# A graph layer with bucketed edges: the first and the last level of ranks as two levels of 64 ranks each

## The chip, the cores and the metric

One core of one Trainium2 chip runs the kernel. The metric is the device time of one execution in microseconds (us), the median of several runs. Engines are named as the profile names them: PE (TensorE matmul) and PEld (its weight loads), DVE (VectorE), ACT (ScalarE), POOL (GpSimd), SP (SyncE, which issues most DMAs).

## The reference

12,500 nodes with 64 features; 212,500 edges (100,000 random pairs in both directions and a loop at each node), sorted by `dst`. `h` is the layer norm of `x` with a relu. For every edge

```
e = silu(silu([h[src], h[dst], dist] @ eW1 + eb1) @ eW2 + eb2)      # 129 -> 128 -> 128
```

The sums of `e` over the edges of one source node form `agg`, and the output is

```
x + silu([h, agg] @ nW1 + nb1) @ nW2 + nb2
```

All of it is float32.

## The kernel before

The edges come sorted by `dst`, but the sums go by `src`. So the kernel sorts them into buckets through DRAM. Node `l * 100 + b` belongs to bucket `b` of 100, and a bucket has 125 nodes. Four buckets are a quad (`G = 4`); there are 25 quads.

**Sending.** The edges are taken in 208 blocks of 1024. For each block, `count` finds on DVE and PE which rank each edge has within its bucket (running totals stand in the PSUM tile `full`), and `send` makes the part of the first layer that belongs to `dst` and the distance (matmul `qp`, L427; copies to `qs` on ACT, L437 and L443). Eight indirect DMAs a block, issued by POOL (L450), then scatter the rows to the DRAM array `q`: a row of 144 floats for each edge (128 values, then the place of its source node within the bucket), at quad, rank, bucket. A block goes out in three pieces (`PIECES`). `qs` has eight buffers, two a block.

**Levels.** Each bucket has room for 2304 ranks. `LEVELS` cuts them into levels: an entry `(n, end, spare)` is a level of n x 128 ranks for every bucket, which is full when block `end` has been sent. `spare` slots of it may be left empty and are zeroed (`fill`); later rows of a bucket that is behind are then moved past the level's end. There are 12 levels: the first is `(1, 18, 0)`, the last `(1, 208, 128)`.

**Steps.** When a level is full, its rows are read back quad by quad (`fetch`: one DMA for `qt`, one for `a`, the table rows of the quad's nodes; four buffers each, `NQ = 4`). A level with n = 2 takes two steps for a quad, one with n = 1 takes one. A step handles four tiles of 128 rows; where n = 1, tile t is bucket t of the quad. It consists of:

- `s_lr` (L526): the rows' node places, spread over partitions (PE, four bf16 matmuls); `s_one_t` (L531): the one-hot matrix `oneT` from them (DVE);
- `s_pt` (L540, L546): the rows turned by four transposes, and the source part `a` added through `oneT` by matmuls; then silu (ACT, L550). Each float32 matmul is two instructions on PE;
- `s_bias` and `s_p2` (L572, L578): the bias copied to PSUM (ACT), the second layer (PE), silu (ACT, L582);
- `s_one` (L559): the one-hot matrix `one` the other way round (DVE); at its end the next `fetch` is issued;
- `s_seg` (L592): the sums of the bucket by a matmul with `one`, into the PSUM tile `seg`, of which there is one buffer;
- `s_add` (L601, L603): `seg` copied or added to `aggT` (DVE).

There are 450 steps. After a quad's last step, `nodes` computes its output rows (`z`, L246 and L249; `o`, L255; `os`, L258) and SP stores them.

**Order.** PE, DVE, ACT and SP execute in the order in which the program is written; no scheduler moves anything. First come preparation and the first blocks. When all pieces of `goal_of(0)` are written, the loop over steps begins. One turn of it follows this list; the number is how many steps ahead (or back) each part works:

```
turn = [
    (s_pt, 1), (s_add, -2), (s_one_t, 2), None, (s_bias, 1), (s_p2, 0), (s_one, 0), None, (s_seg, -1), None, (s_lr, 3), None,
]
```

At each `None` (a hook) pieces of the sending, of the node tables still to be made (`feed`) and of finished quads are written. How many pieces of the sending are due is a straight line between marks; there is a mark at the first fetch of each level, by which the blocks of that level and three more must have been written:

```
LEAD = 3 * PIECES
total = PIECES * (nblocks - 2 * FIRST)
goal_of = lambda w: min(PIECES * (LEVELS[w][1] - 2 * FIRST) + LEAD, total)
```

With `FIRST = 4`, `goal_of(0)` is 39 pieces, which ends block 21; the total is 600. The first fetch of a level also waits on the chip for the landing of the level's last rows (`last_rows`).

Of the kernel before, what the change touches and what calls it, by code (L numbers as in the profile page):

```python
# [28 lines left out]
F32 = mybir.dt.float32  # L29
# [3 lines left out]
AF = mybir.ActivationFunctionType  # L33
OP = mybir.AluOpType
# [4 lines left out]
P = 128  # L39
L = 125  # L40
# [11 lines left out]
G = 4  # L52
W = 144
EPS = 1e-5

LEVELS = [(1, 18, 0), (1, 32, 0), (2, 58, 32), (2, 79, 96), (2, 101, 96), (2, 123, 96), (2, 145, 96), (2, 165, 128)]
LEVELS += [(1, 184, 0), (1, 194, 32), (1, 202, 96), (1, 208, 128)]
ENDS = [P * sum(n for n, _, _ in LEVELS[: w + 1]) for w in range(len(LEVELS))]
SURE = [end - spare for end, (_, _, spare) in zip(ENDS, LEVELS)]
ROWS = ENDS[-1]  # L60
CAP = ROWS // P
# [12 lines left out]
def tile_gnn(ctx: ExitStack, tc: tile.TileContext, x, src, dst, ew, eW1, eb1, eW2, eb2, nW1, nb1, nW2, nb2, out):  # L74
    nc = tc.nc
    N, D = x.shape
    H = eW2.shape[0]
# [97 lines left out]
    nc.vector.scalar_tensor_tensor(same, plus, -32.0, part, op0=OP.mult, op1=OP.add)  # L175
    nc.vector.tensor_scalar(plus, same, float(WL + 1), None, op0=OP.is_equal)
    nc.vector.scalar_tensor_tensor(same, plus, -1e6, same, op0=OP.mult, op1=OP.add)
    ones = const.tile([1, P], F32, name="ones")
    nc.vector.memset(ones, 1.0)
    before = const.tile([P, P], BF16, name="before")  # L180
# [88 lines left out]
    with ExitStack() as work:  # L269
# [199 lines left out]
        last_rows = {}  # L469
# [12 lines left out]


        batches = [(w, B, n) for w, (n, _, _) in enumerate(LEVELS) for B in range(NB // G)]
        steps = [(w, B, n, g) for w, B, n in batches for g in range(n)]
        PIECES = 1 + TB // G
        pending = [needed.count(w) for w in range(len(LEVELS))]
        batch, st = {}, {}

        most = max(n for _, _, n in batches)  # L490

        def fetch(i):
            if i >= len(batches):
                return
            c, B, n = batches[i]
            assert not any(pending[: c + 1])
            while B not in done_a:
                next(feed)
            at = B * G * ROWS + G * (ENDS[c] - n * P)
            qt = ld2.tile([P, G * most, W], F32, name="qt")  # L500
            ins = nc.sync.dma_start(
                qt[:, : G * n, :].rearrange("p j w -> p (j w)"),
                q[at : at + G * n * P, :].rearrange("(p j) w -> p (j w)", p=P),
            ).ins
            for later in range(c + 1, len(LEVELS)):
                tc.declare_no_dep(ins, group=f"rows{later}", reason="these ranks were full before")
            tc.add_manual_dep(ins, last_rows[LEVELS[c][1] - 1].name, AFTER)
            tc.add_to_no_dep_group("loads", ins)
# [19 lines left out]

        def s_one_t(k):
            oneT = wk.tile([L, G, P], F32, name="oneT")  # L530
            nc.vector.tensor_scalar(oneT, st[k].pop("lr")[:L], part1[:L, :], None, op0=OP.is_equal)  # L531
            st[k]["oneT"] = oneT

        def s_pt(k):

            (qt, a, _), tiles = of(k)
            oneT = st[k].pop("oneT")
            pt = mm.tile([P, G, P], F32, name="pt", tag="mm")
            for t, (j, _) in enumerate(tiles):
                nc.tensor.matmul(  # L540
                    pt[:, t, :], qt[:, j, :H], ident, is_transpose=True, start=t == 0, stop=False, skip_group_check=True
                )
            for b, same in itertools.groupby(range(G), lambda t: tiles[t][1]):
                same = list(same)
                cols = slice(same[0], same[-1] + 1)
                nc.tensor.matmul(  # L546
                    pt[:, cols, :], a[:L, b, :], oneT[:, cols, :], start=False, stop=True, skip_group_check=True
                )
            e1 = wk.tile([P, G, P], F32, name="e1")
            nc.scalar.activation(e1, pt, AF.Silu)  # L550
            st[k]["e1"] = e1

        def s_one(k):
            (qt, _, _), tiles = of(k)
            c, B, n, g = steps[k]
            wide = [P, G // n, n, L]
            loc = qt[:, : G * n, H : H + 1].rearrange("p (j b) w -> p b j w", b=G)
            one = wk.tile([P, G, L], F32, name="one")
            nc.vector.tensor_tensor(  # L559
                one.rearrange("p (b j) l -> p b j l", j=n),  # L560
                nodes1[:, None, None, :].to_broadcast(wide),
                loc[:, tiles[0][1] : tiles[0][1] + G // n].to_broadcast(wide),
                op=OP.is_equal,
            )
            st[k]["one"] = one
            if g == n - 1:
                fetch(c * (NB // G) + B + NQ)

        def s_bias(k):

            p2 = p2p.tile([P, G, H], F32, name="p2")
            nc.scalar.copy(p2, b2f)  # L572
            st[k]["p2"] = p2

        def s_p2(k):
            e1, p2 = st[k].pop("e1"), st[k].pop("p2")
            for t in range(G):
                nc.tensor.matmul(  # L578
                    p2[:, t, :], e1[:, t, :], w2, start=False, stop=t == G - 1, skip_group_check=True
                )  # L580
            e2 = wk.tile([P, G, H], F32, name="e2")
            nc.scalar.activation(e2, p2, AF.Silu)  # L582
            st[k]["e2"] = e2

        def s_seg(k):
            c, B, n, g = steps[k]
            item, tiles = of(k)
            if g == 0:
                item[2] = sgp.tile([P, G, L], F32, name="seg")
            e2, one = st[k].pop("e2"), st[k].pop("one")  # L590
            for t, (j, b) in enumerate(tiles):
                nc.tensor.matmul(item[2][:, b, :], e2[:, t, :], one[:, t, :], start=j < G, stop=j >= G * (n - 1))  # L592

        def s_add(k):
            c, B, n, g = steps[k]
            if g < n - 1:
                return
            v = aggT[:, B * G : B * G + G, :]
            seg = batch.pop((c, B))[2]
            if c == 0:  # L600
                nc.vector.tensor_copy(v, seg)  # L601
            else:
                nc.vector.tensor_tensor(v, v, seg, op=OP.add)  # L603
            if c == len(LEVELS) - 1:
                tails.append(nodes(B, *node_in.pop(B), mm, ndp[1], "mm"))
# [465 lines left out]
```

## Time and profile before

| | |
|---|---|
| median of 9 runs | 3059.62 us (3042.93 to 3077.78) |
| profiled execution | 3050.87 us, of which its span is 3049.0 us |
| granted TensorE clock, mean | 0.859 of full speed |
| busy share of the span | PE 76%, PEld 65%, DVE 64%, POOL 56%, ACT 36% |
| float32 matmul instructions of the steps | L546 2400, L578 3600, L592 3600 |
| indirect DMAs of the sending (L450) | 1661, on POOL 1691.9 us in all |
| reads of `qt` (L501) | 150 of 576 KB, 150 of 288 KB |

The profile gives, for each line and engine, the number of instructions, their busy time and what ended the idle time before them. A window view gives the same for a stretch of the span, with the granted clock and the DMA share. The span was seen to fall into these stages: preparation and the first blocks (0 to 281 us), steps with a dense stream of blocks (281 to about 773), the long middle, and the end, in which no block is sent any more (from about 2873).

### The profile page before, as it was taken

What the parts mean: (1) busy time and instruction counts of PE and PEld (TensorE: products, weight loads), DVE (VectorE), ACT (ScalarE), POOL (GpSimd) and SP (SyncE); (2) the same over time, 40 slices, a digit from 0 to 9 for tenths busy, and PEclk for the clock granted to TensorE, in tenths of its full rate; (3) what the DMA queues carried; (4) which work ended last, traced back from release to release, by engine and by line L of the source; (5) the groups of instructions that cost most, each with busy time, mean ns of one, the idle gap of its engine ahead of it and who ended that gap; (6) DMA issues with size and microseconds to landing.
All of it is one profiled execution on the core that took longest, in us unless ns stands there. A gap on an engine that the chain in (4) does not pass through costs nothing.

```text
span 3049.0 us, 46228 instructions
## 1 busy us (share of the span) xinstructions
PE 2305.2 (76%) x16191; PEld 1978.1 (65%) x16191; DVE 1955.4 (64%) x3005; ACT 1085.5 (36%) x2403; POOL 1721.0 (56%) x1712
## 2 busy tenths in 40 slices
PE   3754666555687777877777878887888888888997
PEld 2542565444576666666666766776776777778986
DVE  7654566555666666666667756666776677666643
ACT  2432222222233333333333333343444444334443
POOL 5666566666666566566566656655565665543210
PEclk9655787776799888898899888898999999989999
DMA  4543345444555544455443334333344444445652
GB/s 107 182 145 121 121 147 161 145 139 146 174 178 179 183 145 145 163 182 178 138 135 124 134 119 135 123 130 132 130 141 136 132 136 148 143 150 158 191 159 86
DMA packets 237005, 443.83 MB, mean 146 GB/s; under 512 B 49804, under 2 KB 108735, under 8 KB 236561
## 3 DMA queue, kind: packets, MB, share of 16 engines
q1 hardware_dynamic: 158629, 269.79, 28.0%
q0 software_dynamic: 53536, 123.03, 11.7%
q10 hardware_dynamic: 24602, 47.98, 5.3%
q8 instruction: 131, 2.15, 0.3%
q14 instruction: 107, 0.88, 0.1%
HBM read 251.07 MB, written 189.55 MB: 145 GB/s over the span
## 4 chain that ended last, share of the span: by engine, by line
PE 39%; issue 14%; DVE 13%; POOL 12%; another core or an unknown queue 9%; DMA 3%; ACT 2%; SPq 0%; POOLq 0%; DVEq 0%; ACTq 0%
POOL q L450 12%; PE seg L592 8%; PE p L578 8%; PE pt L546 8%; PE qp L427 5%; PE pt L540 4%; DVE each L362 2%; PE lr L526 2%; DVE oneT L531 2%; DVE oh L354 2%; DVE mine L402 2%; DVE one L559 1%; DVE aggT L603 1%; DVE rank L404 1%
## 5 line engine op out<-in xcount | busy, mean ns | idle before, releaser
L450 POOL DMA_INDIRECT q<-qs,to x1661 | 1691.9, 1019 | 1161.1 <-ACT qs L443 636.5
L592 PE MATMUL seg<-one,e 128*128 128x125 f32 x3600 | 550.3, 297 | 186.8 <-issue 77.2
L550 ACT ACTIVATE e<-pt 128x512 f32<-128x512 f32 x450 | 270.3, 601 | 1077.8 <-PE pt L546 310.2
L592 PEld LDWEIGHTS seg<-one,e 128*128 128x128 f32 x3600 | 487.0, 208 | 238.9 <-issue 190.5
L578 PE MATMUL p<-w,e 128*128 128x128 f32 x3600 | 546.1, 293 | 94.8 <-issue 53.4
L578 PEld LDWEIGHTS p<-w,e 128*128 128x128 f32 x3600 | 495.2, 204 | 165.6 <-issue 90.9
L531 DVE TENSOR_SCALAR oneT<-lr,part 125x512 f32<-125x512 f32 x450 | 336.0, 747 | 411.2 <-remote 160.9
L546 PE MATMUL pt<-oneT,a 125*128 125x128 f32 (+1 forms) x2400 | 526.4, 353 | 37.7 <-issue 34.7
L546 PEld LDWEIGHTS pt<-oneT,a 125*128 125x128 f32 x2400 | 392.6, 211 | 66.4 <-issue 44.7
L603 DVE TENSOR_TENSOR aggT<-aggT,seg 128x500 f32<-128x500 f32 x275 | 184.6, 671 | 342.8 <-remote 157.5
L437 ACT COPY qs<-qp 128x512 f32<-128x512 f32 x416 | 225.8, 589 | 482.0 <-PE qp L427 150.5
L582 ACT ACTIVATE e<-p 128x512 f32<-128x512 f32 x450 | 270.9, 602 | 239.6 <-remote 114.7
L427 PEld LDWEIGHTS qp<-win,pick 64*128 64x128 f32 x1662 | 186.6, 222 | 254.5 <-issue 200.6
L427 PE MATMUL qp<-win,pick 64*128 64x256 f32 x1662 | 310.5, 474 | 40.7 <-issue 27.4
L540 PE MATMUL pt<-ident,qt 128*128 128x128 f32 x1800 | 312.6, 300 | 29.8 <-issue 19.5
L362 DVE TENSOR_REDUCE each<-oh 128x100 bf16<-128x800 bf16 x208 | 315.4, 1516 | 7.2
L559 DVE TENSOR_TENSOR one<-nodes,qt 128x500 f32<-128x500 f32 x450 | 301.9, 671 | 0.0
L402 DVE TENSOR_TENSOR mine<-oh,full 128x800 f32<-128x800 bf16 x208 | 204.0, 981 | 112.0 <-remote 46.0
L572 ACT COPY p<-b2f 128x512 f32<-128x512 f32 x450 | 269.3, 599 | 0.0
L540 PEld LDWEIGHTS pt<-ident,qt 128*128 128x128 f32 x1800 | 213.6, 155 | 69.2 <-issue 46.9
L526 PE MATMUL lr<-identb,qt 128*125 128x128 bf16 x1800 | 199.1, 235 | 61.9 <-issue 42.7
L526 PEld LDWEIGHTS <-qt 128*125 128x125 bf16 x1800 | 173.3, 148 | 102.4 <-issue 89.6
(144 smaller groups left out, 1378.7 us busy)
## 6 DMA issues: line engine op xcount, KB each, us to landing
qt<-q SPq DMA_DIRECT2D x150, 576.0 KB
a<-ta SPq DMA_DIRECT2D x300, 256.0 KB
qt<-q SPq DMA_DIRECT2D x150, 288.0 KB
q<-zeros ACTq DMA_DIRECT2D x25, 1080.0 KB
q<-qs,to POOLq DMA_INDIRECT x1661
q<-zeros ACTq DMA_DIRECT2D x10, 1440.0 KB
bc<-dests SPq DMA_DIRECT2D x103, 128.0 KB
win<-tb SPq DMA_DIRECT2D x416, 30.0 KB
```

The costliest lines, as they stand in the source:

```text
L362: nc.vector.tensor_reduce(each, oh.rearrange("p t b -> p b t"), AX.X, OP.add)
L427: nc.tensor.matmul(qps[i][:, t, : n_of[t]], pick[at, t * P : (t + 1) * P], win[at, : n_of[t]], start=True, stop=True)
L450: ins = nc.gpsimd.indirect_dma_start(out=q[:], out_offset=bass.IndirectOffsetOnAxis(ap=to[:k, j : j + 1], axis=0), in_=qs[:k, t, a, :], in ...
L526: nc.tensor.matmul(lr[:L, t, :], loc[:, at : at + 1].to_broadcast([P, L]), identb, start=True, stop=True)
L531: nc.vector.tensor_scalar(oneT, st[k].pop("lr")[:L], part1[:L, :], None, op0=OP.is_equal)
L540: nc.tensor.matmul(pt[:, t, :], qt[:, j, :H], ident, is_transpose=True, start=t == 0, stop=False, skip_group_check=True)
L546: nc.tensor.matmul(pt[:, cols, :], a[:L, b, :], oneT[:, cols, :], start=False, stop=True, skip_group_check=True)
L550: nc.scalar.activation(e1, pt, AF.Silu)
L559: nc.vector.tensor_tensor(one.rearrange("p (b j) l -> p b j l", j=n), nodes1[:, None, None, :].to_broadcast(wide), loc[:, tiles[0][1] : ti ...
L578: nc.tensor.matmul(p2[:, t, :], e1[:, t, :], w2, start=False, stop=t == G - 1, skip_group_check=True)
L582: nc.scalar.activation(e2, p2, AF.Silu)
L592: nc.tensor.matmul(item[2][:, b, :], e2[:, t, :], one[:, t, :], start=j < G, stop=j >= G * (n - 1))
```

## The change

The first level becomes `(0.5, 11, 0), (0.5, 18, 0)`, the last `(0.5, 205, 64), (0.5, 208, 64)`: there are 14 levels. A level with n = 0.5 has 64 ranks of every bucket. A step of it takes one whole quad, 256 rows, in two tiles. Tile j holds bucket j on partitions 0 to 63 and bucket 2 + j on partitions 64 to 127. So `fetch` reads `qt` in two DMAs, one for each half of the partitions; `a` is read as before. `s_lr`, `oneT`, the transposes, the silus, the bias copy and the second layer work on two tiles instead of four. In `s_pt` the source part is added by four matmuls of 64 columns. For the sums, the new constant `nodes2` holds the node numbers on one half of the partitions and -1 on the other; so `one` has four blocks as before, each with zeros for the half of the partitions that belongs to another bucket, and `s_seg` keeps its four matmuls (two tiles, each used with two blocks of `one`). `s_add` and the fetch of `a` happen once for each level and quad, so for 50 quads more than before. `goal_of` is unchanged.

```diff
-LEVELS = [(1, 18, 0), (1, 32, 0), (2, 58, 32), (2, 79, 96), (2, 101, 96), (2, 123, 96), (2, 145, 96), (2, 165, 128)]
-LEVELS += [(1, 184, 0), (1, 194, 32), (1, 202, 96), (1, 208, 128)]
-ENDS = [P * sum(n for n, _, _ in LEVELS[: w + 1]) for w in range(len(LEVELS))]
+LEVELS = [(0.5, 11, 0), (0.5, 18, 0), (1, 32, 0), (2, 58, 32), (2, 79, 96), (2, 101, 96), (2, 123, 96), (2, 145, 96), (2, 165, 128)]
+LEVELS += [(1, 184, 0), (1, 194, 32), (1, 202, 96), (0.5, 205, 64), (0.5, 208, 64)]
+ENDS = [int(P * sum(n for n, _, _ in LEVELS[: w + 1])) for w in range(len(LEVELS))]
...
+    mid = const.tile([P, 2], F32, name="mid")
+    nc.vector.tensor_scalar(mid[:, 0:1], part, P / 2 - 0.5, None, op0=OP.is_lt)
+    nc.vector.tensor_scalar(mid[:, 1:2], part, P / 2 - 0.5, None, op0=OP.is_gt)
+    nodes2 = const.tile([P, 2, L], F32, name="nodes2")
+    for h in range(2):
+        nc.vector.tensor_scalar(nodes2[:, h, :], nodes1, 1.0, mid[:, h : h + 1], op0=OP.add, op1=OP.mult)
+    nc.vector.tensor_scalar(nodes2, nodes2, -1.0, None, op0=OP.add)
...
-        steps = [(w, B, n, g) for w, B, n in batches for g in range(n)]
+        steps = [(w, B, n, g) for w, B, n in batches for g in range(max(1, n))]
...
+            rows = G * int(n * P)
+            at = B * G * ROWS + G * ENDS[c] - rows
             qt = ld2.tile([P, G * most, W], F32, name="qt")
...
+            if n < 1:
+                parts = q[at : at + rows, :].rearrange("(r h j) w -> h r (j w)", h=2, j=2)
+                loads = [(qt[h * 64 : h * 64 + 64, :2, :], parts[h]) for h in range(2)]
+            else:
+                loads = [(qt[:, : G * n, :], q[at : at + rows, :].rearrange("(p j) w -> p (j w)", p=P))]
+            for to, part_ in loads:
+                ins = nc.sync.dma_start(to.rearrange("p j w -> p (j w)"), part_).ins
...
             c, B, n, g = steps[k]
+            if n < 1:
+                return batch[c, B], [(0, None), (1, None)]
...
-            nc.vector.tensor_scalar(oneT, st[k].pop("lr")[:L], part1[:L, :], None, op0=OP.is_equal)
+            nt = len(of(k)[1])
+            nc.vector.tensor_scalar(oneT[:, :nt], st[k].pop("lr")[:L, :nt], part1[:L, :], None, op0=OP.is_equal)
...
+            for j, h in itertools.product(range(nt), range(2)) if n < 1 else ():
+                cols = slice(h * 64, h * 64 + 64)
+                nc.tensor.matmul(
+                    pt[:, j, cols], a[:L, 2 * h + j, :], oneT[:, j, cols], start=False, stop=True, skip_group_check=True
+                )
...
+            if n < 1:
+                wide = [P, 2, 2, L]
+                j, of_nodes = 2, nodes2[:, :, None, :]
+                loc = qt[:, None, :2, H : H + 1]
...
-            if g == n - 1:
+            if g == max(1, n) - 1:
                 fetch(c * (NB // G) + B + NQ)
...
+            for b in range(G) if n < 1 else ():
+                nc.tensor.matmul(item[2][:, b, :], e2[:, b % 2, :], one[:, b, :], start=True, stop=True)
...
-            by = sum(x[2] for x in batches[: start + 1]) - 2
+            by = sum(max(1, x[2]) for x in batches[: start + 1]) - 2
```

More of the change, by code (lines that the diff above doesn't have):

```diff
@@ L488, in tile_gnn @@
         batch, st = {}, {}
-        most = max(n for _, _, n in batches)
+        most = max(max(1, n) for _, _, n in batches)
         def fetch(i):
@@ L498, in fetch @@
                 next(feed)
-            at = B * G * ROWS + G * (ENDS[c] - n * P)
+            rows = G * int(n * P)
+            at = B * G * ROWS + G * ENDS[c] - rows
             qt = ld2.tile([P, G * most, W], F32, name="qt")
[L501 to L508, printed above, removed]
+            if n < 1:
[5 more added lines that the diff above has]
+                ins = nc.sync.dma_start(to.rearrange("p j w -> p (j w)"), part_).ins
+                for later in range(c + 1, len(LEVELS)):
+                    tc.declare_no_dep(ins, group=f"rows{later}", reason="these ranks were full before")
+                tc.add_manual_dep(ins, last_rows[LEVELS[c][1] - 1].name, AFTER)
+                tc.add_to_no_dep_group("loads", ins)
             a = ld2.tile([P, G, H], F32, name="a")
@@ L542, in s_pt @@
                 )
-            for b, same in itertools.groupby(range(G), lambda t: tiles[t][1]):
+            nt, n = len(tiles), steps[k][2]
+            for j, h in itertools.product(range(nt), range(2)) if n < 1 else ():
[3 more added lines that the diff above has]
+                )
+            for b, same in itertools.groupby(range(G), lambda t: tiles[t][1]) if n >= 1 else ():
                 same = list(same)
@@ L549, in s_pt @@
             e1 = wk.tile([P, G, P], F32, name="e1")
-            nc.scalar.activation(e1, pt, AF.Silu)
+            nc.scalar.activation(e1[:, :nt], pt[:, :nt], AF.Silu)
             st[k]["e1"] = e1
@@ L555, in s_one @@
             c, B, n, g = steps[k]
-            wide = [P, G // n, n, L]
-            loc = qt[:, : G * n, H : H + 1].rearrange("p (j b) w -> p b j w", b=G)
             one = wk.tile([P, G, L], F32, name="one")
+            if n < 1:
+                wide = [P, 2, 2, L]
+                j, of_nodes = 2, nodes2[:, :, None, :]
+                loc = qt[:, None, :2, H : H + 1]
+            else:
+                wide = [P, G // n, n, L]
+                j, of_nodes = n, nodes1[:, None, None, :]
+                loc = qt[:, : G * n, H : H + 1].rearrange("p (j b) w -> p b j w", b=G)
+                loc = loc[:, tiles[0][1] : tiles[0][1] + G // n]
             nc.vector.tensor_tensor(
[L560 to L563, printed above, removed]
+                one.rearrange("p (b j) l -> p b j l", j=j), of_nodes.to_broadcast(wide), loc.to_broadcast(wide), op=OP.is_equal
             )
             st[k]["one"] = one
-            if g == n - 1:
+            if g == max(1, n) - 1:
                 fetch(c * (NB // G) + B + NQ)
@@ L571, in s_bias @@
             p2 = p2p.tile([P, G, H], F32, name="p2")
-            nc.scalar.copy(p2, b2f)
+            nt = len(of(k)[1])
+            nc.scalar.copy(p2[:, :nt], b2f[:, :nt])
             st[k]["p2"] = p2
@@ L576, in s_p2 @@
             e1, p2 = st[k].pop("e1"), st[k].pop("p2")
-            for t in range(G):
+            nt = len(of(k)[1])
+            for t in range(nt):
                 nc.tensor.matmul(
-                    p2[:, t, :], e1[:, t, :], w2, start=False, stop=t == G - 1, skip_group_check=True
+                    p2[:, t, :], e1[:, t, :], w2, start=False, stop=t == nt - 1, skip_group_check=True
                 )
             e2 = wk.tile([P, G, H], F32, name="e2")
-            nc.scalar.activation(e2, p2, AF.Silu)
+            nc.scalar.activation(e2[:, :nt], p2[:, :nt], AF.Silu)
             st[k]["e2"] = e2
@@ L590, in s_seg @@
             e2, one = st[k].pop("e2"), st[k].pop("one")
-            for t, (j, b) in enumerate(tiles):
+            for b in range(G) if n < 1 else ():
+                nc.tensor.matmul(item[2][:, b, :], e2[:, b % 2, :], one[:, b, :], start=True, stop=True)
+            for t, (j, b) in enumerate(tiles if n >= 1 else ()):
                 nc.tensor.matmul(item[2][:, b, :], e2[:, t, :], one[:, t, :], start=j < G, stop=j >= G * (n - 1))
@@ L595, in s_add @@
             c, B, n, g = steps[k]
-            if g < n - 1:
+            if g < max(1, n) - 1:
                 return
```

## The prediction

> **What bounds the kernel now.** First the page: no engine fills the span, so the bound has to be looked for by stage.
>
> ```profile
> PE   3754666555687777877777878887888888888997
> ...
> POOL 5666566666666566566566656655565665543210
> PEclk9655787776799888898899888898999999989999
> ```
>
> PE ends at nine tenths and full clock while POOL goes idle; in the first quarter POOL is steady at five or six tenths and the clock is low. The window view cuts this (PE, PEld, DVE, ACT, POOL busy; clock; DMA share; GB/s):
>
> ```profile
> 184.00:270.00 86.00, 46.90 (x246) 34.12 (x248) 53.68 (x83) 26.20 (x79) 56.37 (x57) 0.58 0.39 132
> 270.00:451.00 181.00, 109.60 (x706) 91.90 (x704) 98.56 (x147) 48.36 (x109) 112.20 (x112) 0.73 0.44 135
> 451.00:773.00 322.00, 184.35 (x1068) 151.23 (x1068) 187.35 (x284) 75.28 (x178) 203.21 (x205) 0.72 0.47 147
> ...
> 2893.00:3005.00 112.00, 112.00 (x915) 98.83 (x914) 44.69 (x77) 46.21 (x95) 13.79 (x19) 1.00 0.52 164
> ```
>
> The edges are block starts on POOL (block 11 starts at 184, 18 at 270, 32 at 451, 58 at 773; eight indirect DMAs a block). The pace is 12.3, 12.9 and 12.4 us a block: the same with no step beside the blocks as with one step per block. POOL's own pitch between indirect DMAs is 1.27 us (trace), so 10.2 us a block; the waits of POOL for 40 to 773 us fill the rest:
>
> ```profile
> POOL q L450 <- issue: 125.1, 409, 0.5
> POOL q L450 <- ACT qs L443: 125.0, 26, 22.9
> ```
>
> So up to block 58 the chain of sending sets the time. After 2893 it is PE alone: 112 busy in 112 us. The timeline of one late turn without node work gives the pitches:
>
> ```profile
> 2889.00 0.39 PE L526 MATMUL lr<-identb,qt 128*125 128x128 bf16 x4
> 2889.20 0.67 DVE L603 TENSOR_TENSOR aggT<-aggT,seg 128x500 f32<-128x500 f32 x1 [1.43 <-PE seg L592]
> 2889.23 0.61 PE L540 MATMUL pt<-ident,qt 128*128 128x128 f32 x4
> 2889.68 1.06 PE L546 MATMUL pt<-oneT,a 125*128 125x128 f32 x8
> 2889.80 0.74 DVE L531 TENSOR_SCALAR oneT<-lr,part 125x512 f32<-125x512 f32 x1
> 2890.46 0.67 DVE L559 TENSOR_TENSOR one<-nodes,qt 128x500 f32<-128x500 f32 x1
> 2890.57 1.06 PE L578 MATMUL p<-w,e 128*128 128x128 f32 x8
> 2891.19 0.34 SPq L501 DMA_DIRECT2D qt<-q  x1
> 2891.46 1.05 PE L592 MATMUL seg<-one,e 128*128 128x125 f32 x8
> 2892.35 0.39 PE L526 MATMUL lr<-identb,qt 128*125 128x128 bf16 x4
> ...
> 3008.41 0.98 PE L255 MATMUL o<-w2n,zs 128*125 128x64 f32 x8
> 3009.23 1.11 PE L592 MATMUL seg<-one,e 128*128 128x125 f32 x8
> ```
>
> From start to start, PE spends 0.23 on `lr`, 0.45 on the transposes, and 0.89 each on `a`, `p` and `seg`: 3.35 us a step. With a quad's node work turns repeat every 5.89 us (`oneT` starts of the last 20 steps). The last two lines are for later: eight passes of 64 columns took 0.82.
>
> **The change, part by part.** The sum is made against the profiled execution, 3050.87 us (span 3049.0 and 1.9 around it), and the difference is added to the median, 8.75 above it.
>
> *Half a step on PE.* Two `lr` 0.12, two transposes 0.22, `p` in four passes 0.45, `seg` still eight passes 0.89. The source part is eight passes of 64 columns: no row has them in this place, the nearest is `o` with 64 columns and a weight tile as wide, 0.82 against 0.89. I take 0.82, so half a step costs 2.50 us; two cost 1.65 more than the whole one. If half the columns took half the time (0.45) it would be 2.13.
>
> The Trainium skill's page "TensorE: Matmul & The Clock Gate" (Back-to-back issue gap) has a start-to-start of N/2.4 + 2.5 ns for isolated matmuls, 29 ns at 64 columns, and warns that a stream with weight loads is spaced by both. By the formula `a` would cost 0.23, half a step 1.91, and the end below would lose 28 us in place of 44. The 0.82 of `o` decides for the warning.
>
> *The end.* Does the first half of the last level start earlier? By `goal_of`, no: the level that ends at 205 wants 3 x (205 - 8) + 9 = 600 pieces before its first fetch, which is all of them, as the last level did before. So the last blocks go out beside the level of 202 as now, PE was busy 88 of 89 us there (2786 to 2875), and behind it stand 50 half steps in place of 25 steps. Nothing of the end is moved forward; work is added.
>
> The 25 half steps without node work have PE's 2.50 or the loop that a fetch closes: `add` to the issue of `qt` is 1.99 in the timeline (2889.20 to 2891.19), less 0.32 for half of `oneT` (`os`, 256 columns, took 0.425 against 0.747); the second `qt` is issued 0.34 later; the landing takes 2.80 (288 KB, trace) or, nearest in size, 2.14 (`hd`, 128 KB). With 0.2 from `lr` to `add` that is 4.35 to 5.0 for two turns, 2.2 to 2.5 each. Both limits almost meet, so 2.6: 65 us. The 25 with node work: 5.89 - 3.35 + 2.50 = 5.04, which saves 0.85 x 25 = 21. Sum +44. Low end: with 2.13, level 205 is held by the loop, 2.5 x 25 = 63, and the other saves 1.22 x 25 = 31: +32. High end: if the waits pull the clock to the 0.72 of 451 to 773, 2.50 becomes 3.5: 87 - 21 = +66.
>
> By the same page (Part 1: The HAM clock gate) the clock halves only after about 3.4 us of idleness, longer than any wait here, which would leave 44; no run yet shows such turns.
>
> *The start.* The first fetch waits for block 11's rows and not block 18's: steps start near 192 instead of 281. But emission is coupled: from whole step 17 on, the straight line between marks gives each step the same number of written blocks as before (33.7 after step 17, and after step 42 with 25 more). So only blocks 11 to 32 change. *Blocks 11 to 18* took 86 us with no steps; now 23 half turns lie among them. Low end 86 (the blocks' pace holds). From the steps: the nearest stage with n = 1 and few blocks, steps 350 to 375 (2523 to 2654), took 5.26 a turn with 0.36 blocks at a clock of 0.95. PE's work per turn there is 3.35 + 0.36 x 1.4 = 3.85 (eight `qp` and two `full` are about 1.4), here 2.50 + 0.30 x 1.4 = 2.92: 4.0 a turn, and 5.1 at 0.74 of the clock, 118 for 23. Between the ends I take 4.5, 104: +18. *Blocks 18 to 32* took 181 with 25 whole steps among them; with half steps I take 12.5 a block, 175: -6. Ends: 160 (11.4 a block, half of the wait gone) and 181. Sum of the start +12, from -21 to +32.
>
> *At no cost.* `mid` and `nodes2`: five small DVE operations ahead of the first blocks, 1.2 us if nothing hides them, taken as 1. The 50 additional `add` and `one` (0.67 each) lie beside PE at the end and count in the DVE share of the half turns; if DVE were the bound of blocks 11 to 18 (0.67 + 0.43 + 0.67 + 0.3 x 5.5 = 3.4 a turn) they stay under 4.5. SP gets 50 further reads of `a` and 100 of `qt`, 0.34 to 0.38 each, at most 1.1 us in a 2.6 us turn, with node work 3.1 in 5.04; behind the waiting fetch stand the loads for blocks to come, written three blocks ahead, so a late one costs POOL nothing until about 30 us. The middle is the same program.
>
> Total: 44 + 12 + 1 = +57: 3108 for a run like the profiled one, 3117 for the median.
>
> **The rivals.**
> *Faster, from the head start.* 89 us of earlier steps take PE work out of the stretch in which blocks and steps collide. Price: blocks 11 to 32 at POOL's own 10.2 us take 214 for 267, -53; with the formula's end of +28, -25: 3035. It decides from below about 10.6 us a block (267 - 44, over 21 blocks). Against it: the same 12.3 us a block where there are no steps at all.
> *No change.* Cheap half steps (+28) and 11.4 us a block from 18 to 32 (-21): +7, 3067. It needs both ends.
> *Much slower.* Clock 0.72 in the half turns (+66) and 118 us for blocks 11 to 18 (+32): +99, 3159.
> *It does not do what it says.* A bucket with fewer than 64 ranks after block 11 would send the kernel into the general path. Counted from the inputs, the smallest has 89, so this gets no chance.
>
> **How the numbers follow.** Forecast, +57 with its neighbours from +20 to +85: 0.62. Much slower 0.10. No change 0.18, of which 0.05 is slower by over 0.5% and 0.13 within. Faster 0.10, of which 0.01 is within. Half a per cent, 15 us, is about what a measurement of this kernel can tell from no change. Faster 0.09, same 0.14, slower 0.77. The range reaches from no change (3063) to near the much slower case (3150).
>
> **What would show it.** Last indirect DMA at about 2882 and after it some 190 us of turns (144 before); turns of about 2.6, then 5.0 us; `a` with 64 columns at 0.1 us a pass; first `oneT` near 205; block 32 between 430 and 485. Wrong would be: steps of level 205 before the last block, half steps near 2 us, or block 32 before 420.

## The result and the profile after

The changed kernel took 3158.19 us in the median, beside 3053.88 us for the kernel before: a ratio of 1.0345 (95% interval 1.0323 to 1.0367). The ratio is taken over the fast runs alone, the medians over all. That is 104 us where 57 were forecast, and outside the range. The profiled execution has a span of 3159.4 us against 3049.0.

The page after, in the same three rows:

```profile
PE   3767765556677777878877787788788888779998
...
POOL 5655566666666655666656565656656665442010
PEclk8559777777889888888989898988899999989998
```

The foot of POOL is longer: more of the span lies behind the last block. The last indirect DMA came at 2919.6 us (2869.3 before); behind it lie 239.7 us (179.7 before). So 60 of the 110 us between the two profiles are the end. The window view of after, cut at the same blocks (11 at 186, 18 at 295, 21 at 344, 32 at 488, 58 at 810), and two windows of the end:

```profile
186.00:295.00 109.00, 77.03 (x559) 65.08 (x558) 63.46 (x107) 39.80 (x117) 58.64 (x57) 0.78 0.51 163
295.00:344.00 49.00, 35.45 (x247) 31.07 (x247) 31.36 (x52) 12.75 (x40) 24.34 (x25) 0.85 0.40 120
344.00:488.00 144.00, 97.93 (x567) 84.98 (x566) 91.65 (x145) 33.62 (x102) 89.81 (x89) 0.70 0.43 128
488.00:810.00 322.00, 189.34 (x1106) 156.50 (x1106) 193.37 (x297) 74.39 (x189) 206.76 (x209) 0.73 0.48 152
...
2930.00:2996.00 66.00, 62.94 (x580) 62.11 (x579) 39.62 (x73) 24.10 (x72) 0.00 (x0) 1.00 0.53 149
3005.00:3110.00 105.00, 104.22 (x777) 88.37 (x777) 41.94 (x81) 34.46 (x97) 15.25 (x21) 1.00 0.54 156
```

Blocks 11 to 18 took 109 us (86 before), 18 to 21 took 49 (37), 21 to 32 took 144 (145), 32 to 58 took 322 (328): block 58 starts 31 us late, though the first step came 77 us earlier (first `oneT` at 218 instead of 295). At the end PE is nearly as full as before (62.9 of 66 and 104.2 of 105 us) and the clock is 1.00. What POOL waited for up to block 58 has changed little in kind; added are waits for ACT while it works for the tables (`rows_a`, 21.9 for 3.9 before) and for the steps (`p`):

```profile
POOL q L457 <- issue: 127.2, 416, 0.5
POOL q L457 <- ACT qs L450: 123.1, 25, 22.7
POOL q L457 <- ACT rows_a L214: 21.9, 4, 10.9
POOL q L457 <- ACT p L597: 19.8, 3, 10.2
```

One half turn at the end without node work, from the timeline of after:

```profile
2962.08 1.09 SPq L515 DMA_DIRECT2D qt<-q  x2
...
2962.73 0.28 PE L539 MATMUL lr<-identb,qt 128*125 128x128 bf16 x2
2962.84 0.39 PE L554 MATMUL pt<-ident,qt 128*128 128x128 f32 x2
2962.93 0.67 DVE L631 TENSOR_TENSOR aggT<-aggT,seg 128x500 f32<-128x500 f32 x1 [0.92 <-PE seg L618]
2963.07 1.00 PE L560 MATMUL pt<-oneT,a 125*128 125x64 f32 x8
2963.53 0.48 DVE L545 TENSOR_SCALAR oneT<-lr,part 125x256 f32<-125x256 f32 x1
2963.91 0.66 PE L604 MATMUL p<-w,e 128*128 128x128 f32 x4
2963.92 0.67 DVE L586 TENSOR_TENSOR one<-nodes,qt 128x500 f32<-128x500 f32 x1
2964.41 1.05 PE L618 MATMUL seg<-one,e 128*128 128x125 f32 x8
...
2965.30 0.28 PE L539 MATMUL lr<-identb,qt 128*125 128x128 bf16 x2
```

PE goes from `lr` to `lr` in 2.57 us: 0.11, 0.23, 0.84 from `a` to `p`, 0.50 and 0.89. And a half turn with node work, in which PE stands still ahead of `o` and within it; the first line below is of before:

```profile
3007.41 1.16 PE L578 MATMUL p<-w,e 128*128 128x128 f32 x8
...
3060.73 1.06 PE L253 MATMUL z<-aggT,w1g 128*128 128x250 f32 x4
3061.73 0.69 PE L256 MATMUL z<-hrn,w1n 64*128 64x250 f32 x4
3062.35 0.71 PE L604 MATMUL p<-w,e 128*128 128x128 f32 x4
3062.45 0.83 ACT L258 ACTIVATE zs<-z,nb1c 128x250 f32<-128x250 f32 x2 [1.14 <-PE z L256]
3062.97 1.23 PE L262 MATMUL o<-w2n,zs 128*125 128x64 f32 x8
3064.03 1.11 PE L618 MATMUL seg<-one,e 128*128 128x125 f32 x8
```

From start to start `p` took 0.62 us and `o` 1.06. Before, `p` took 1.00 (3007.41 to 3008.41) and `o` 0.82; with four passes of 0.11 fewer, `p` alone would take 0.55.

### The profile page after: what moved, and what is told of

Its sections match the earlier page's. It is cut to its first block, busy times and chain, and to the rows that moved or that the text cites. A ratio compares the mean times of both kernels' runs of the same rounds, so it can differ in the third digit from the quotient of the medians.

```text
span 3159.4 us, 48733 instructions
## 1 busy us (share of the span) xinstructions
PE 2410.8 (76%) x16991; PEld 2075.4 (66%) x16991; DVE 2028.9 (64%) x3170; ACT 1105.8 (35%) x2553; POOL 1726.6 (55%) x1712
## 4 chain that ended last, share of the span: by engine, by line
PE 36%; DVE 15%; issue 13%; another core or an unknown queue 11%; POOL 11%; DMA 4%; ACT 2%; SPq 0%; DVEq 0%; POOLq 0%; ACTq 0%
POOL q L457 11%; PE p L604 7%; PE pt L566 6%; PE seg L620 6%; PE qp L434 4%; PE pt L554 4%; DVE oneT L545 2%; DVE each L369 2%; PE lr L539 2%; DVE oh L361 2%; DVE one L586 2%; PE seg L618 2%; DVE mine L409 2%; DMA q<-qs,to 2%
## 5 line engine op out<-in xcount | busy, mean ns | idle before, releaser
L570 ACT ACTIVATE e<-pt 128x512 f32<-128x512 f32 (+1 forms) x500 | 279.1, 558 | 1188.4 <-remote 345.8
L620 PE MATMUL seg<-one,e 128*128 128x125 f32 x3200 | 483.6, 295 | 172.8 <-DVE aggT L631 75.5
L545 DVE TENSOR_SCALAR oneT<-lr,part 125x512 f32<-125x512 f32 (+1 forms) x500 | 346.5, 693 | 416.0 <-PE lr L539 136.5
L620 PEld LDWEIGHTS seg<-one,e 128*128 128x128 f32 x3200 | 429.4, 207 | 220.4 <-issue 183.9
L566 PE MATMUL pt<-oneT,a 125*128 125x256 f32 (+1 forms) x2000 | 464.6, 363 | 27.3 <-issue 24.2
L631 DVE TENSOR_TENSOR aggT<-aggT,seg 128x500 f32<-128x500 f32 x325 | 218.4, 672 | 407.8 <-remote 187.4
L566 PEld LDWEIGHTS pt<-oneT,a 125*128 125x128 f32 x2000 | 334.0, 209 | 59.7 <-issue 34.1
L608 ACT ACTIVATE e<-p 128x512 f32<-128x512 f32 (+1 forms) x500 | 279.9, 560 | 226.3 <-remote 63.0
L586 DVE TENSOR_TENSOR one<-nodes,qt 128x500 f32<-128x500 f32 x500 | 335.9, 672 | 0.0
L597 ACT COPY p<-b2f 128x512 f32<-128x512 f32 (+1 forms) x500 | 277.6, 555 | 0.0
L554 PEld LDWEIGHTS pt<-ident,qt 128*128 128x128 f32 x1800 | 209.4, 153 | 91.0 <-issue 62.9
```

Source lines behind the costliest of these rows:

```text
L545: nc.vector.tensor_scalar(oneT[:, :nt], st[k].pop("lr")[:L, :nt], part1[:L, :], None, op0=OP.is_equal)
L554: nc.tensor.matmul(pt[:, t, :], qt[:, j, :H], ident, is_transpose=True, start=t == 0, stop=False, skip_group_check=True)
L566: nc.tensor.matmul(pt[:, cols, :], a[:L, b, :], oneT[:, cols, :], start=False, stop=True, skip_group_check=True)
L570: nc.scalar.activation(e1[:, :nt], pt[:, :nt], AF.Silu)
L586: nc.vector.tensor_tensor(one.rearrange("p (b j) l -> p b j l", j=j), of_nodes.to_broadcast(wide), loc.to_broadcast(wide), op=OP.is_equal)
L608: nc.scalar.activation(e2[:, :nt], p2[:, :nt], AF.Silu)
```

## The experiments

The result and the four groups of kernels below come from five chips, and these differ: the kernel before took 3054 us beside the result and 3091, 3051, 2497 and 3102 beside the groups (in the order of the table: first_only to one_load, before_again to early_ends, code_only to feed_first, after_again to feed_first2). So ratios are compared with ratios, and traces by stretches. "14 to 21" is the time between the starts of these blocks on POOL, "middle" the time from block 58 to the last block, "end" what follows the last indirect DMA.

| kernel | ratio (95%) | 14 to 21 | 21 to 32 | block 58 at | middle | end |
|---|---|---|---|---|---|---|
| before | | 85 | 145 | 779 | 2090 | 180 |
| after | 1.0345 (1.0323 to 1.0367) | 112 | 144 | 810 | 2110 | 240 |
| first_only | 1.0138 (1.0093 to 1.0183) | 104 | 145 | 813 | 2134 | 180 |
| last_only | 1.0211 (1.015 to 1.0271) | 86 | 149 | 781 | 2125 | 239 |
| o_late | 1.0292 (1.0224 to 1.0359) | 110 | 145 | 817 | 2142 | 237 |
| one_load | 1.0451 (1.0402 to 1.0499) | 122 | 149 | 832 | 2132 | 278 |
| before_again | | 86 | 142 | 775 | 2081 | 180 |
| parity | 1.0265 (1.0216 to 1.0314) | 104 | 142 | 798 | 2104 | 233 |
| no_head | 1.0209 (1.0175 to 1.0243) | 143 | 147 | 833 | 2128 | 180 |
| early_ends | 0.9956 (0.9922 to 0.999) | 87 | 144 | 778 | 2074 | 180 |
| code_only | 1.0003 (0.9989 to 1.0017) | 72 | 116 | 663 | 1651 | 182 |
| pe_cut | 1.0217 (1.0186 to 1.0247) | 75 | 118 | 665 | 1655 | 227 |
| dve_cut | 1.0215 (1.0188 to 1.0242) | 73 | 115 | 658 | 1653 | 237 |
| feed_first | 1.0241 (1.0216 to 1.0266) | 79 | 118 | 669 | 1652 | 240 |
| after_again | 1.0253 (1.021 to 1.0295) | 106 | 145 | 808 | 2130 | 240 |
| pe_cut2 | 1.0231 (1.0157 to 1.0306) | 109 | 151 | 823 | 2131 | 230 |
| dve_cut2 | 1.0331 (1.0259 to 1.0403) | 117 | 151 | 828 | 2130 | 236 |
| feed_first2 | 1.03 (1.0241 to 1.0358) | 106 | 145 | 811 | 2133 | 239 |

**One split at a time.**

```diff
-LEVELS += [(1, 184, 0), (1, 194, 32), (1, 202, 96), (0.5, 205, 64), (0.5, 208, 64)]
+LEVELS += [(1, 184, 0), (1, 194, 32), (1, 202, 96), (1, 208, 128)]      # first_only
```
```diff
-LEVELS = [(0.5, 11, 0), (0.5, 18, 0), (1, 32, 0), (2, 58, 32), (2, 79, 96), (2, 101, 96), (2, 123, 96), (2, 145, 96), (2, 165, 128)]
+LEVELS = [(1, 18, 0), (1, 32, 0), (2, 58, 32), (2, 79, 96), (2, 101, 96), (2, 123, 96), (2, 145, 96), (2, 165, 128)]  # last_only
```

> Only the first level is split, the last is (1, 208, 128) as before. If the two splits add up, this costs what the trace of after shows up to the last block: block 58 about 31 us late (779 to 810 us) and the last indirect DMA about 31 to 50 us late, with the end as before (turns of 5.9 us, 180 us from the last block to the end of the span): +31 to +50, 3085 to 3104 for the median. If the 14 to 19 us that after loses between block 58 and the last block come from the split at the end or are chance, it is 3085; if they come from the start, 3099. My prediction had +13 for this half, 3067.

> Only the last level is split, the first is (1, 18, 0) as before. Everything up to the last block as before (last indirect DMA within 10 us of 2869), then 240 us to the end of the span instead of 180: +60, 3114 for the median. My prediction had +44 for this half, 3098. If the loss between block 58 and the last block came from the split at the end, this would show 3130.

Both lose, each at its own place: first_only has block 58 at 813 and the old end, last_only the old start and an end of 239. The ratios add to 1.035, the ratio of after.

**The output matmuls one hook later.**

```diff
             nc.scalar.activation(zs[:, a], z[a], AF.Silu, bias=nb1c)
         yield
+        yield
...
         nc.vector.tensor_tensor(os_, o, xr, op=OP.add)
-        yield
```

> The changed kernel with the output matmuls of a finished quad (o) one hook later, behind the sums of the step, and the store with the addition. Theory: in the half turns with node work PE waits 0.38 us because four passes of the second layer no longer cover the silu of z on ACT (5.42 us a turn, the sum was 5.04). Then these 24 turns take 5.05 us and the time falls by 9 us against the changed kernel, to about 3149. Rival: the 0.38 is PE's own work at another pitch; then the turn stays at 5.4 and the time at 3158.

The node turns went from 5.43 to 5.25 us (median of the last 15), the end from 240 to 237: a third of the 9 us expected. By the rows of this trace `o` is back at 0.82, `p` at 0.55 and `seg` at 0.89, 0.37 less in all, but `a`, which now follows `o` more closely, takes 0.98 for 0.84, and `z` 0.05 more; so moving `o` wins 0.18 of the 0.39 a turn by which the sum was too small. The ratio can't tell 3 us.

**One load for a half step, twice.** First with the two halves of the partitions in one DMA:

```diff
-                parts = q[at : at + rows, :].rearrange("(r h j) w -> h r (j w)", h=2, j=2)
-                loads = [(qt[h * 64 : h * 64 + 64, :2, :], parts[h]) for h in range(2)]
+                both = q[at : at + rows, :]
+                both = bass.AP(tensor=both.tensor, offset=both.offset, ap=[[2 * W, 2], [4 * W, 64], [1, 2 * W]])
+                loads = [(qt[:, :2, :], both)]
```

> The changed kernel with the rows of a half step read by one DMA over all 128 partitions in place of two over 64. The two took 1.09 us of SP a turn, one of twice the size 0.34. If SP's own time or the later landing of the second part holds the half turns at the start, blocks 11 to 32 take 10 us less or more than that (302 us in after), and the time falls to 3145 or below. If the start is held by the turns themselves (order of PE, ACT and DVE), block 32 stays within 5 us of 488 us and the time within 5 us of 3158.

Its ratio is 1% above that of after, and it taught what the fetch does to the turns. Its timeline in level 205:

```profile
3001.83 0.33 PE L540 MATMUL lr<-identb,qt 128*125 128x128 bf16 x2 [1.14 <-DMA qt<-q]
...
3003.33 0.51 SPq L516 DMA_DIRECT2D qt<-q  x1
...
3005.75 0.33 PE L540 MATMUL lr<-identb,qt 128*125 128x128 bf16 x2 [1.14 <-DMA qt<-q]
```

PE now waits for `qt`, and the turn is 3.92. The load is issued 1.5 us after an `lr` (3003.33) and releases the `lr` two turns on (3009.66), 6.33 later; the last of its semaphore updates comes 6.28 after the issue (median in level 205). So 1.5 + 6.33 is two turns of 3.92: the loop that the prediction described, with its price. In the trace 2.0 packets of 1152 bytes were in flight on average while any were; in parity, below, 8.6. This agrees with what the Trainium skill's page "DMA: Bandwidth & Descriptors" (Why a DMA increments its semaphore by 16 and not by 1) says of the engines that a DMA uses: their number divides the slowest dimension of both of its access patterns, and that of the source is 2 here. The suspicion against SP's issue time was not tested by this kernel, since the landing changed with it.

Then with the buckets on even and odd partitions, so that the rows lie in DRAM as the partitions take them:

```diff
-    nc.vector.tensor_scalar(mid[:, 0:1], part, P / 2 - 0.5, None, op0=OP.is_lt)
-    nc.vector.tensor_scalar(mid[:, 1:2], part, P / 2 - 0.5, None, op0=OP.is_gt)
...
+    nc.vector.tensor_scalar(mid[:, 0:1], low2, 0.5, None, op0=OP.is_lt)
+    nc.vector.tensor_scalar(mid[:, 1:2], low2, 0.5, None, op0=OP.is_gt)
...
+                loads = [(qt[:, :2, :], q[at : at + rows, :].rearrange("(p j) w -> p (j w)", p=P))]
...
-                cols = slice(h * 64, h * 64 + 64)
+                cols = slice(h, P, 2)
```

> The changed kernel with the two buckets of a tile on even and odd partitions in place of the two halves. The rows of a half step then lie in DRAM in the order of the partitions, and one DMA of 144 KB loads them in the form in which the other levels are loaded. Theory: the loop closed by the fetch is two turns, so the turn is half of (1.5 us + landing); with one load that lands in 2.3 us and 0.34 us of SP instead of 1.09 the half turns of level 205 are PE's 2.57 throughout (2.80 on average in after) and the end is 5 us shorter; the start gains 0 to 10 us, since its turns are at 5.3 us, twice what this loop needs. In all 1.029 to 1.033 of before. If SP's issue time is what holds the start, blocks 11 to 32 fall from 302 to below 285 us and the ratio to 1.025 or less. If columns with a stride of two cost PE more, the turns are above 2.57.

```profile
2939.91 0.32 SPq L519 DMA_DIRECT2D qt<-q  x1
```

One load, 0.32 of SP for 1.09. Level 205 fell from 2.80 to 2.61 us a step, the end from 240 to 233; blocks 11 to 32 took 294 us (302 in after), above the 285 that would have made SP's time the cause. Columns with a stride of two cost PE nothing (turns of 2.57). So the two loads are 7 us of the end, and perhaps 8 of the start, which is no more than repetitions of the same start differ (14 to 21: 104 to 112). The ratio, 1.0265, lies below the 1.029 to 1.033 expected and above the 1.025 of the rival; with no run of after on this chip it settles nothing.

**No head start, and a head start without half steps.**

```diff
-LEVELS = [(0.5, 11, 0), (0.5, 18, 0), (1, 32, 0), (2, 58, 32), (2, 79, 96), (2, 101, 96), (2, 123, 96), (2, 145, 96), (2, 165, 128)]
-LEVELS += [(1, 184, 0), (1, 194, 32), (1, 202, 96), (0.5, 205, 64), (0.5, 208, 64)]
+LEVELS = [(0.5, 18, 0), (0.5, 18, 0), (1, 32, 0), (2, 58, 32), (2, 79, 96), (2, 101, 96), (2, 123, 96), (2, 145, 96), (2, 165, 128)]
+LEVELS += [(1, 184, 0), (1, 194, 32), (1, 202, 96), (1, 208, 128)]  # no_head
```

> First level as two of 64 ranks, but both full only at block 18, so that no step starts earlier than before; the last level is (1, 208, 128). Blocks 11 to 18 then go out without steps (86 us in before) and 50 half turns lie where 25 whole turns lay. Theory A: a half turn beside blocks costs some 5 us by itself (the order that PE, ACT and DVE share), wherever it lies: the 46 half turns until block 35 is written take 46 x 5.3 = 244 us from about 281, block 32 comes near 500 to 510 (451 in before, 488 in first_only) and the ratio is 1.015 to 1.02. Theory B: the half turns of first_only were slow because the node tables were still being made beside them; then block 32 is at 470 or earlier and the ratio at 1.01 or below.

Block 32 came at 511 and the ratio fits theory A, but not for its reason. Both marks want the same 39 pieces, so no block is written during the first 20 steps, which the expectation had overlooked: POOL waits (blocks 18 to 21 took 94 us), and the 25 half turns run alone.

```profile
271.00:365.00 94.00, 67.26 (x554) 64.47 (x551) 42.16 (x76) 27.01 (x80) 23.18 (x25) 0.80 0.48 132
```

They took 3.03 us each (first `oneT` 296, the 26th 372). Beside blocks the same 25 took 5.3 in after. While POOL sends nothing at all (307 to 364), PE is busy for 54.0 of 57 us and the clock is 0.99. Block 58 is at 833 (775 in before_again on this chip, 813 in first_only on another); how much of that is the missing head start and how much the stretch in which POOL had nothing to send, this kernel can't tell.

```diff
-LEVELS = [(1, 18, 0), (1, 32, 0), (2, 58, 32), (2, 79, 96), (2, 101, 96), (2, 123, 96), (2, 145, 96), (2, 165, 128)]
-LEVELS += [(1, 184, 0), (1, 194, 32), (1, 202, 96), (1, 208, 128)]
+LEVELS = [(1, 17, 0), (1, 30, 0), (2, 55, 32), (2, 76, 96), (2, 99, 96), (2, 121, 96), (2, 143, 96), (2, 164, 128)]
+LEVELS += [(1, 183, 0), (1, 193, 32), (1, 202, 96), (1, 208, 128)]
```

> The kernel before with whole levels, but each level taken as full one to three blocks earlier (17, 30, 55, 76, 99, 121, 143, 164, 183, 193, 202, 208), as far as the counts of the inputs allow; no operation is added. Theory: up to block 58 the sending sets the time and PE has room, so steps moved there are nearly free, and PE, which bounds the rest, has fewer left: three blocks at level 55 are about 3 to 7 steps, 10 to 35 us: ratio 0.989 to 0.997. Rival: each block beside more steps takes longer by what the steps cost, as in the half levels: no change, 0.998 to 1.005.

This one is faster than both kernels, by 0.44% (0.1 to 0.78%), about 13 us: the first step at 275 instead of 295, block 58 where it was (778), the middle 2074 instead of 2081. So steps moved forward without new work cost little or nothing, as the prediction read the start; the two profiles alone (3 us more to block 58, 7 less in the middle) differ no more than repetitions do. (The ends fit these inputs; others could need the general path.)

**The unchanged program.**

> The kernel before, unchanged, for a profile on the chip on which the other kernels of this group run. In the trace of after, 14 to 19 us were lost between block 58 and the last block, where the program is the same; in the kernels with one split that stretch took 2125 and 2134 us, against 2090 in the trace of before and 2110 in that of after. Theory: this is chip and run, no part of the change; then the kernel before takes 2110 to 2135 here too. Rival: the split does it; then it takes about 2090.

It took 2081, which spoke for the split. But this profile was 13 us under its chip's median (3051), no_head's 28 over its own; with both brought to the median the middle of before is 2094 there and that of no_head and parity 2100. On the chips of first_only and after_again no profile of before was taken; if block 58 and the end stand there as in the other profiles of before, its median leaves an estimated 2132 and 2141 for the middle, as much as the split kernels had. So some 12 of the 104 us are left for the middle, and whether the split causes any of them stayed open.

> The code of after with the 12 levels of before: nodes2 is made, every step is whole, no level is split. In the traces the stretch from block 58 to the last block is 10 to 30 us longer wherever a level is split, although the program there is the same. If the new constants (their place in SBUF, five DVE operations) did that, this shows 1.003 to 1.006; if not, 0.998 to 1.002.

1.0003: the new constants cost nothing.

**What holds the half turns at the start.** Three suspects, each taken away alone.

```diff
-            for j, h in itertools.product(range(nt), range(2)) if n < 1 else ():
-                cols = slice(h * 64, h * 64 + 64)
+            for j, h in itertools.product(range(nt), range(1)) if n < 1 else ():
+                cols = slice(0, P)                                      # pe_cut
```
```diff
-                wide = [P, 2, 2, L]
-                j, of_nodes = 2, nodes2[:, :, None, :]
+                wide = [P, 1, 2, L]
+                j, of_nodes = 2, nodes2[:, :1, None, :]
...
-                nc.tensor.matmul(item[2][:, b, :], e2[:, b % 2, :], one[:, b, :], start=True, stop=True)
+                nc.tensor.matmul(item[2][:, b, :], e2[:, b % 2, :], one[:, b % 2, :], start=True, stop=True)  # dve_cut
```
```diff
             next(pieces)
-            for _ in range(3):
+            for _ in range(5):
                 next(feed, None)                                        # feed_first
```

> The changed kernel with two matmuls of 128 columns for the source part of a half step in place of four of 64 (the table rows of two of the four buckets are left out). Eight passes become four, the columns stay the same. If a pass costs the same with 64 columns as with 128 (0.111 us in after), the half step at the end falls from 2.57 to about 2.3, where the loop of the fetch holds it, and the end is 15 to 18 us shorter; if half the columns cost half, nothing changes. At the start: if PE holds the half turns beside the blocks (16 us a block from block 14 to 21, 9.9 of them PE at full clock), these 7 blocks take 10 us less (112 in after); if DVE does, under 5 us less.

> The changed kernel with the one-hot matrix of a half step made for two of the four buckets (half of the DVE operation; the sums of the other two take the same half). DVE falls by 0.3 us a half turn. At the end PE holds, so level 205 stays at 2.6 to 2.8 us and the end within 6 us of 240. At the start: DVE was busy 11.5 of 16 us a block there, 72%, the same share as in the long middle (9.6 of 13.4); if it holds, blocks 14 to 21 take 7 to 10 us less than 112; if PE or the order of the turns does, under 4 us less.

> The changed kernel with five instead of three items of the node tables per piece before the steps, so that the tables are finished before the first half turn instead of in the first three turns. If the tables beside the half turns cost the start something (8 us more from block 11 to 14 than in before, POOL waiting 14.5 us for the copies of table rows), block 21 comes 5 to 10 us earlier than 344 us; if the items only change places, within 4 us of 344, with blocks 8 to 11 later.

At the end pe_cut gave 227 us (feed_first on this chip 240), 13 less where 15 to 18 were expected, with node turns of 5.23 instead of 5.43 and level 205 at 2.50, not 2.3. A pass of 64 columns costs what one of 128 costs: the passes of `a` follow each other by 0.111 us (median) in after and by 0.112 in pe_cut. But at the start this chip had little to tell, as there blocks 14 to 21 took 72 us in code_only (POOL's own pitch makes 71) and 73 to 79 with half steps beside them. So the three ran again beside the changed kernel:

> The changed kernel once more, beside the three others of this group on one chip. On the chip of the group before, the kernel before took 2497 us and not some 3050, and there the start cost at most 7 us (blocks 14 to 21: 79 against 72) and the end 58. Theory: the end costs 58 to 60 us on every chip, the start costs 25 to 30 us only where the hand-offs between engines come late. So a ratio of 1.024 to 1.027 if this chip is as quick, 1.03 to 1.035 if it is like the first; blocks 14 to 21 about 78 or about 110.

> As pe_cut (source part of a half step in four passes of 128 columns, two buckets' table rows left out), to be compared with after_again on the same chip. End 12 us shorter than after_again. If PE's work sets the half turns of the start, blocks 14 to 21 are 8 us or more shorter; if the hand-offs between engines do, under 5, since their number is the same.

> As dve_cut (half of the one-hot operation left out, two buckets' sums with it), beside after_again on the same chip. End within 4 us of after_again. If DVE's work sets the half turns of the start, blocks 14 to 21 are 7 us or more shorter; if the hand-offs do, under 5.

> As feed_first (the node tables finished before the first half turn), beside after_again on the same chip. If the tables beside the first half turns are part of the cost, blocks 11 to 21 take 5 us less or more than that; if not, within 4 us of after_again.

Here blocks 14 to 21 took 106 us in after_again, and 109, 117 and 106 with PE, DVE or the tables relieved: none of the three alone sets them. (Blocks 11 to 21 took 6 us less in feed_first2, 150 for 156, which by its expectation would speak for the tables; but block 11 came 6 us later and block 21 at 342 in both, so the items only changed places.) The ratio of after_again, 1.0253, is below that of after with an interval that does not touch; the price differs by chip, and its end does not (239 or 240 on four chips, last_only and feed_first among them). The theory on record had this ratio for a chip with 78 us for blocks 14 to 21 and got it with 106: block 58 at 808 (775 to 781 where the first level is whole, on the other chips of this pace) shows the price of the start here too. By the estimate above the middle is some 11 us shorter than that of before, which is not explained.

What is left is the hand-off between engines. The chain of the page points to it, in before and in code_only on its chip:

```profile
PE 39%; issue 14%; DVE 13%; POOL 12%; another core or an unknown queue 9%; DMA 3%; ACT 2%; SPq 0%; POOLq 0%; DVEq 0%; ACTq 0%
```
```profile
PE 32%; DMA 20%; POOL 15%; DVE 15%; issue 8%; ACT 2%; DVEq 0%; POOLq 0%; ACTq 0%; SPq 0%
```

"Another core or an unknown queue" is no third party: it is an engine that starts long after the end of what it waited for. From the timeline of before:

```profile
447.68 1.05 PE L592 MATMUL seg<-one,e 128*128 128x125 f32 x8
...
449.25 1.06 PE L546 MATMUL pt<-oneT,a 125*128 125x128 f32 x8
...
453.49 0.68 DVE L601 COPY aggT<-seg 128x500 f32<-128x500 f32 x1 [4.15 <-remote]
...
463.68 0.60 ACT L550 ACTIVATE e<-pt 128x512 f32<-128x512 f32 x1 [13.73 <-remote]
```

The sums ended at 448.7, their copy starts at 453.5; `pt` ended at 450.3, its silu starts at 463.7. In the trace's record of semaphores, 844 of 2728 updates by PE in before come more than 1 us after the recorded end of the matmul, in code_only 8. (A tenth of these records is missing in before, so that the first count is somewhat high; counted back from each update that is recorded it is some 600. The late starts of the waiting engines are not touched by that: 198 waits, 892 us in all, end with such a start in before, none in code_only.)

The traces also show when hand-offs are late: only while blocks are sent. After the last indirect DMA, none of the 210 hand-offs of PE in before is late and none of the 363 in after (count by the next recorded update, over 1 us). That fits an end that costs the same on every chip. In no_head none of the 102 between 307 and 364 us is late, where POOL sends nothing, but 51 of 121 are between 375 and 511. On the chip of code_only, where hand-offs are prompt, the 25 half turns took 3.9 us each beside blocks (feed_first), between the 3.0 of no_head and the 5.3 of after.

A half turn passes as many results from engine to engine as a whole one, and there are 25 more turns at the start. That late hand-offs make their price is argued from the three cuts, from no_head and from the chip without them, where the start cost 6 us or less (block 58 in feed_first, pe_cut and dve_cut against code_only). No run delayed or hastened a hand-off by itself: no_head took the blocks' own work away with the sending, and the other comparison is between chips. So it is not shown, and what about the sending makes hand-offs late, and why not on every chip, stayed open.

## Why the prediction was wrong

**Right:** the direction; that the last level's first half would not start earlier, so that the end only gets longer; that block 58's time would not fall with the head start; the loop of the fetch and its formula; that 64 columns are not half the price of 128; that the blocks from 21 on go at the pace of the sending (of the two waits of POOL that it shows, only that for `qs` fills the rest of a block: the 0.3 us of `issue` at each DMA are part of the pitch of 1.27). Block 58 of before starts at 779 and not at 773, which moves no term.

Of the 47 us that the sum lacks, 16 are the end's, 19 the start's and some 12 the middle's.

**The end, +44 forecast, +60 measured** (high end +66). The mechanism held; terms of the sum were too small. Level 205: 2.80 us a step for 2.6, because two DMAs of 64 partitions take SP 1.09 us and land late now and then (parity: 2.61); 5 us. Level 208, from its first `oneT` to the end of the span, took 159.4 for 169.3, a saving of 10 where 21 were summed. Its node turn is 5.43 and not 5.04, and the rows account for the 0.39: `p` no longer covers the silu of `z`, so PE waits ahead of `o` (0.08 us) and within it (0.24), a wait that had no term; and `a` gave nothing (0.07). The few turns of the level without node work, which the sum had overlooked, saved about half a us each and not 0.85.

A smaller step failed on PE, that 64 columns in place of 128 make `a` cheaper, 0.82 for 0.89: `a` and the four passes of `p` behind it took 0.84 and 0.50, 0.112 a pass, for a summed 0.82 and 0.45. The row of `o` was the right one to take, but of its eight passes the first is short (0.055 to the next start, the others 0.11), and what it lacks stands in the first pass of `seg` behind it (0.16). The Trainium skill's page "TensorE: Matmul & The Clock Gate" (LDWEIGHTS) has a weight load take time by its columns, for 128 an estimate of 107 ns by its formula. The float32 rows are near that; the bf16 rows of `lr`, 0.056 a pass with 125 columns of weights, are below it, so that the weight load is the reason is not shown here.

**The start, +12 forecast, +31 measured** (high end +32). The step that failed is the 4.5 us for a half turn beside blocks, with the place that the sum gave these turns; 25 of them took 5.3 each. The sum put 23 among blocks 11 to 18 and let the blocks from 18 on run at 12.5 us each. But by `goal_of` no step is written before block 14 is out: the first `oneT` came at 218, not near 205, 15 started before block 18 and 9 more between 18 and 21. So blocks 11 to 18 took 109 for 104, and blocks 18 to 32 took 193 for 175: the -6 was +12, all of it before block 21, since from 21 to 32 they took 144 us as before. I scaled a late stage by PE's work, and the cuts show that neither PE's work nor DVE's alone sets these turns. The 5.1 of the high end is near the 5.3, but by luck, since it was made of PE's work at a low clock.

**The range.** The "much slower" case, 3159, had the right time by luck: its two conditions did not hold (the clock was 1.00 at the end, and blocks 11 to 18 took 109 us and not 118), and some 12 us of the 104 lie in the middle, which it did not touch. It had 0.10, and I cut the range at 3150, below it. I had taken the two high ends for independent; but at both places a whole step's row was scaled by PE's work, and at both what does not scale came on top. The 12 us of the middle, if they are real, had no term at all.

## What to carry to other kernels

Halving a step does not halve its cost. On PE only what has half the passes became cheaper here (`lr`, the transposes, `p`); `a` kept its eight passes and took 0.84 for 0.89 with half the columns. Eleven operations, an `add`, a DMA's landing and all hand-offs stayed, and the step cost 2.57 of 3.35 us on PE. A finer split can pay only where the start it brings forward was the bound; look first at what the order of emission permits (`goal_of` was already at its limit), and look for a version that moves the same work without more of it, as early_ends did. And when a step gets shorter, ask what its long part was covering.

## What was not expected of the hardware

The same program took 2497 us on one chip and 3051 to 3102 on the others, with equal durations of its operations (a pass 0.111 us, an `oneT` 0.75). What the traces show to differ is the time between the end of an operation and the start of the one that waits for it: 0.01 us at the median and the 90th percentile of PE's updates there, 0.16 and 3.2 in before, and in before only while indirect DMAs go out (none of 210 after the last one is over 1 us). A change that adds steps was 2.1 to 2.4% slower there with parts left out or moved, and 2.5 to 3.5% on the others in full.
